# Where a layernorm's two small scaling steps run in a fused stage, and the order in which that stage issues its work

## The chip, the cores and the metric

The kernel runs on one core of one Trainium2 chip. The metric is the device time of one execution in microseconds. Three runs of the kernel before took 4185.84, 4186.37 and 4202.35 us; their median is 4186.37 us.

A core has five engines that run their own queues in order: TensorE (PE; PEld is its weight load), VectorE (DVE), ScalarE (ACT), GpSimd (POOL) and SyncE (SP), which here issues most DMAs. An instruction that waits for another engine holds up everything behind it in its own queue.

## The reference

The input is 4 sequences of 2048 tokens with 256 features, in float32. Four layers follow, each with a residual and a layernorm without weights ahead of it:

```python
def _layernorm(x, axis=-1, eps=1e-05):
    m = jnp.mean(x, axis=axis, keepdims=True)
    v = jnp.var(x, axis=axis, keepdims=True)
    return (x - m) / jnp.sqrt(v + eps)

x = x + _L0_attn_ref(_layernorm(x), ...)   # RWKV: projections, a scan over time, an FFN
x = x + _L0_ffn_ref(_layernorm(x), ...)    # 2 shared and 16 routed experts, top 4, all computed, gated
x = x + _L1_attn_ref(_layernorm(x), ...)   # Mamba: projections, convolution, selective scan with 16 states
x = x + _L1_ffn_ref(_layernorm(x), ...)    # two groups of 32 experts, top 2, tokens sorted by expert
```

## The kernel before

The tokens are cut into 16 chunks of 512 (4 sequences by 4 pieces), each held as 128 partitions by 4 groups of tokens (S = 4) by 256 features. Three phases follow one another: `rwkv_phase` (the first layer), `mixed_phase` (the second and third layers and the routing of the fourth: the fused stage that the change touches) and `grouped_phase` (the experts of the fourth layer, page by page).

In `mixed_phase` each chunk n goes through three sets of steps. `experts` loads the chunk, normalizes it ("b"), computes router gates, and takes 18 experts in 5 batches: `weights` loads (SP), `up` matmuls (PE), `gelu` (ACT, with a table load before and after), `gated` (a product on POOL), `down` (PE), `added` (DVE). `front` normalizes again ("c"), projects, convolves (`taken` on ACT, `conv` on DVE), and computes the step sizes (`soft` on ACT, `lost` and `dt` on DVE, `less` and `dx` on POOL). `back` runs the selective scan: for g and m in 4 by 4, `enter` forms the inputs c_u on POOL in two halves, `decay` computes one exponential c_da per q on ACT into a PSUM bank, `scan` (L1294) runs the recurrence on DVE in place in c_u, `add` sums over states on PE, `keep` saves the last state on ACT. `steps_in` and `inputs_in` load their inputs through SP. Then `gated` and `out_of` give the layer's output, `summed` (L1330) adds the residual, the chunk is normalized a third time ("w"), and a router with a chain of small DVE steps (`less_max`, `terms`, `largest`, `one_hot`, `rank`, `take_pages`, `place`, `note_pages`, `pick`) finds the row of each token, to which `put` (16 indirect DMAs from POOL) scatters it. In this chain ACT makes small copies: c_np (L1455) in `note_pages` is one that DVE's next step (L1461) waits for, pos_sb (L1483) in `pick` one that `put` waits for.

The order is written out by hand. `MIXED_ORDER` has for each step a list of places, one for each of its instances in a chunk: 456 places in all. Instance i of chunk n is issued at place n * 456 + entry. An entry of -343 is thus issued one chunk's length before the chunk's own start, beside the back of the chunk before. Every engine gets its instructions in this order, so places modulo 456 show what stands next to what once the stage has filled. PSUM banks (8) go round in the order of issue too: a step that takes a bank waits for the reader of the tile that was there. c_u has three buffers.

Each of the three layernorms takes `stats` on DVE (one bn_stats and bn_aggr for each of the 4 groups of tokens), then `scale`, which calls `moments` (L860 to L868): on 128 x 4 numbers it adds epsilon to the variance (rs, L863) and negates the mean (sh, L865) on DVE, then raises rs to the power -0.5 (L866) and multiplies sh by it (L867) on POOL. `normed` (L871) applies both on ACT.

Of the kernel before, what the change touches and what calls it, by code (L numbers as in the profile page):

```python
# [9 lines left out]
F32 = mybir.dt.float32  # L10
I32 = mybir.dt.int32
AF = mybir.ActivationFunctionType
ALU = mybir.AluOpType
# [4 lines left out]
P = 128  # L18
# [3 lines left out]
S = TC // P  # L22
# [6 lines left out]
EPS_LN = 1e-5  # L29
# [20 lines left out]
def bcast_dram(ap, n):  # L50

    run = 1
    for s in ap.shape:
# [4 lines left out]


MIXED_ORDER = {  # L60
    "experts.load": [-1147],
    "b.stats": [-1088, -1083, -1082, -1077],
    "b.normed": [-1054, -1040, -1031, -1032],
    "b.scale": [-1060],
    "b.turn": [-1021, -1018],
    "experts.turned": [-1011, -1002],
    "experts.logit": [-985],
    "experts.logit_out": [-982],
    "experts.logit_turn": [-957],
    "experts.less_max": [-925],  # L70
    "experts.terms": [-921],
    "experts.total": [-914],
    "experts.largest": [-907],
    "experts.taken": [-889],
    "experts.weighted": [-870],
    "experts.gate_turn": [-865],
    "experts.gate_out": [-846],
    "experts.weights": [-860, -852, -800, -755, -714, -648, -639, -608, -516, -419],
    "experts.gates_in": [-810, -764, -685, -624, -500],
    "experts.up": [  # L80
        -830, -816, -815, -735, -748, -720, -719, -652, -642, -635, -631, -541, -540, -579,
        -535, -484, -472, -470,
    ],
    "experts.gelu": [-813, -718, -625, -534, -461],
    "experts.gated": [-793, -1407, -711, -702, -620, -613, -527, -521, -459, -449],
    "experts.down": [
        -787, -783, -768, -759, -681, -672, -657, -645, -595, -589, -577, -567, -504, -497,
        -520, -514, -389, -388, -417, -415,
    ],
    "experts.added": [-757, -747, -663, -641, -572, -552, -476, -482, -369, -395],  # L90
    "c.stats": [-365, -362, -347, -363],
    "c.normed": [-333, -321, -326, -328],
    "c.scale": [-343],
    "c.turn": [-315, -287],
    "front.turned": [-304, -281],
    "front.project": [-273, -259, -260, -243],
    "front.taken": [-265, -238, -226, -219],
    "front.conv": [-254, -252, -250, -234, -230, -227, -223, -221, -213, -209, -206, -198],
    "front.silu_x": [-194],
    "front.b_of": [-153],  # L100
    "front.b_out": [-137],
    "front.dt_of": [-159, -158, -75, -68, 0, 2, 114, 115],
    "front.soft": [-147, -145, -57, -51, 19, 26, 143, 146],
    "front.lost": [-135, -46, 38, 154],
    "front.less": [-131, -36, 51, 156],
    "front.dt": [-122, -31, 78, 172],
    "front.dx": [-115, -23, 142, 217],
    "front.put": [-107, -105, 49, -18, 105, 158, 300, 239],
    "back.b_in": [-37, -129, -101, -72],
    "back.res_of": [20, 29, 14, 22],  # L110
    "back.taken_res": [28, 62, 33, 90],
    "back.silu_res": [170],
    "back.gated": [178, 244, 374, 480],
    "back.steps_in": [-104, -89, 55, 59, 167, 173, 301, 343],
    "back.inputs_in": [-92, -40, 53, 54, 179, 219, 242, 266],
    "back.enter": [
        -1, 36, -8, -7, 27, 76, 79, 86, 106, 108, 132, 134, 151, 162, 187, 188, 232, 248, 224,
        245, 254, 274, 329, 331, 318, 344, 376, 382, 363, 394, 429, 434,
    ],
    "back.decay": [  # L120
# [4 lines left out]
    ],  # L125
    "back.scan": [
# [4 lines left out]
    ],  # L131
    "back.add": [63, 69, 103, 124, 168, 208, 209, 234, 307, 320, 358, 370, 414, 435, 465, 471],
    "back.keep": [72, 81, 104, 118, 159, 215, 228, 251, 310, 305, 353, 373, 418, 444, 469, 473],
    "back.out_of": [567, 577, 488, 506],
    "back.summed": [593, 530],
    "back.store": [638],
    "w.stats": [595, 616, 603, 601],
    "w.normed": [702, 708, 713, 712],
    "w.scale": [679],
    "w.turn": [719, 721],  # L140
    "back.turned": [728, 732],
    "back.logit": [740],
    "back.less_max": [751],
    "back.terms": [758],
    "back.shares": [762],
    "back.largest": [768, 778],
    "back.one_hot": [772, 786],
    "back.count": [817],
    "back.rank": [818],
    "back.take_pages": [825],  # L150
    "back.place_pages": [831],
    "back.note_pages": [846],
    "back.place": [845],
    "back.pick": [853, 859],
    "back.put": [
        856, 863, 869, 908, 946, 970, 983, 987, 1007, 1062, 1078, 1097, 1111, 1115, 1117, 1124,
    ],
}

# [620 lines left out]
def mixed_phase(ctx, tc, cm, nb, nt, x_in, x_out, edge, pos, wgt, xs, w):  # L780
# [11 lines left out]
    nc = tc.nc  # L792
# [13 lines left out]
    wp = ctx.enter_context(tc.tile_pool(name="c_w", bufs=1))  # L806
# [28 lines left out]
    nc.vector.tensor_scalar_mul(am, am, -1.0)  # L835
    one = vp.tile([P, 1], F32, name="c_one")
    nc.vector.memset(one, 1.0)
    few = wp.tile([P, 1], F32, name="c_few")
    nc.vector.memset(few, -0.5)
    past = wp.tile([P, nb, G, NCONV - 1], F32, name="c_past")  # L840
    nc.vector.memset(past, 0.0)
    state = wp.tile([P, nb, G, NM, NC], F32, name="c_state")
# [17 lines left out]
    def moments(mv, name):  # L860

        rs = sm.tile([P, S], F32, name=f"{name}_rs")
        nc.vector.tensor_scalar_add(rs, mv[:, :, 1], EPS_LN)  # L863
        sh = sm.tile([P, S], F32, name=f"{name}_sh")
        nc.vector.tensor_scalar_mul(sh, mv[:, :, 0], -1.0)  # L865
        nc.gpsimd.tensor_tensor(rs, rs, few.to_broadcast([P, S]), ALU.pow)  # L866
        nc.gpsimd.tensor_tensor(sh, sh, rs, ALU.mult)  # L867
        return rs, sh  # L868

# [681 lines left out]
    for n in range(nb * nt):  # L1551
        c = {}
# [227 lines left out]
def layers(tc, nb, nt, w, out):  # L1780
# [5 lines left out]
    with (  # L1786
# [158 lines left out]
```

## Time and profile before

| | before |
|---|---|
| median of three runs | 4186.37 us (4185.84 to 4202.35) |
| the profiled execution | 4192.52 us; span 4190.7 us, clock 0.948 |
| busy share of the span | PE 90%, PEld 50%, DVE 80%, ACT 63%, POOL 76% |
| first phase, 0 to 1190 us | PE busy 1055, DVE 1051, POOL 951, ACT 685 us |
| fused stage once full, 1629 to 2900 us | of 1271 us: PE 1222, DVE 1212, POOL 1186, ACT 1029 us, clock 1.00 |
| last phase, 3550 to 4190 us | of 640 us: PE 545, DVE 281, POOL 264, ACT 194 us; DMA 260 GB/s |

Durations are those of one profiled execution. "Idle before" is time in which the engine stood still ahead of a group of instructions, and the arrow names what ended most of it. Waits that happen inside an instruction count as busy.

### The profile page before, as it was taken

To read this page: it belongs to the slowest core of one execution; us is meant where nothing else is said; L and a number is where in the kernel's file an instruction comes from. 1 tells how busy PE (TensorE), PEld (TensorE's weight loads), DVE (VectorE), ACT (ScalarE), POOL (GpSimd) and SP (SyncE) were. 2 spreads that over 40 slices of the span, in tenths; PEclk is the share of its full clock that TensorE was granted. 3 is DMA by queue.
4 is the path that set the end of the run, shared out by engine and by line. 5 is a ranking of instruction groups with operands and counts; after the bars stand their busy time and mean duration, and the time that the engine had idled before them with its cause. 6 is when DMAs were issued, how large, how long until landed. Compare 5 with 4: busy or idle time off the path is not lost. (4 is left out here: it accounts for less than half of the span.)

```text
span 4190.7 us, 49205 instructions
## 1 busy us (share of the span) xinstructions
PE 3753.3 (90%) x15360; PEld 2102.6 (50%) x15360; DVE 3363.2 (80%) x4824; ACT 2619.9 (63%) x4863; POOL 3182.3 (76%) x1955
## 2 busy tenths in 40 slices
PE   5799999999997999999999999999999764997986
PEld 1244444544454545545455454554545321886875
DVE  6988888888941489999999999999999996354444
ACT  4656556565643688887888778887788762332322
POOL 7978878788721588999999999999999895154245
PEclk8899999999998999999999999999999876999998
DMA  7666666767723555455555555545555334698787
GB/s 209 177 193 165 184 171 163 192 166 188 177 65 126 165 175 190 167 174 178 185 202 169 170 180 185 194 170 177 172 194 178 118 131 166 233 302 307 242 266 227
DMA packets 400259, 774.60 MB, mean 185 GB/s; under 512 B 36416, under 2 KB 238080, under 8 KB 374400
## 3 DMA queue, kind: packets, MB, share of 16 engines
q1 hardware_dynamic: 299280, 612.92, 47.5%
q10 hardware_dynamic: 76144, 91.38, 6.5%
q0 software_dynamic: 24576, 67.14, 4.5%
q8 instruction: 126, 2.06, 0.2%
q14 instruction: 133, 1.09, 0.1%
HBM read 577.32 MB, written 193.99 MB: 184 GB/s over the span
## 5 line engine op out<-in xcount | busy, mean ns | idle before, releaser
L1294 DVE TENSOR_TENSOR_SCAN c_u<-c_da,c_state,c_u 128x512 f32<-128x512 f32 x1024 | 1255.9, 1265 | 51.8 <-ACT c_da L1288 41.6
L1280 POOL TENSOR_TENSOR c_u<-c_dxr,c_bb 128x1024 f32<-128x1024 f32 x512 | 1198.4, 2363 | 36.4 <-ACT c_state L1300 23.3
L1288 ACT ACTIVATE c_da<-c_dtr,c_A 128x512 f32<-128x512 f32 x1024 | 684.4, 686 | 134.3 <-DVE c_u L1294 71.4
L550 POOL TENSOR_TENSOR a_vb<-a_vb,a_k 128x2048 f32<-128x2048 f32 x128 | 579.2, 4538 | 79.7 <-DMA a_vb<-a_vd 78.2
L560 DVE TENSOR_TENSOR_SCAN a_sc<-a_d,a_sc,a_vb 128x512 f32<-128x512 f32 x512 | 623.9, 1265 | 10.5 <-ACT a_sc L556 7.9
L1074 PE MATMUL b_acc<-b_w,b_act 128*128 128x256 f32 x2304 | 543.7, 385 | 22.1 <-POOL b_act L1067 10.9
L1049 PE MATMUL b_pu<-b_y,b_w 128*128 128x512 f32 x1152 | 533.2, 602 | 19.4 <-DVE c_dt L1199 12.6
L1746 POOL DMA_INDIRECT d_y<-d_ys,pos_sb x256 | 247.6, 967 | 364.2 <-DVE d_xt L1645 111.5
L1074 PEld LDWEIGHTS b_acc<-b_w,b_act 128*128 128x128 f32 x2304 | 425.6, 190 | 180.8 <-issue 78.5
L1306 PE MATMUL p_y<-c_u,c_red 128*32 128x512 f32 x2048 | 338.5, 626 | 73.0 <-DVE c_u L1294 54.0
L1067 POOL TENSOR_TENSOR b_act<-b_act,b_gb 128x1024 f32<-128x1024 f32 (+1 forms) x144 | 303.4, 2117 | 107.7 <-ACT b_act L1057 95.4
L1049 PEld LDWEIGHTS b_pu<-b_y,b_w 128*128 128x128 f32 x1152 | 211.3, 190 | 284.9 <-issue 183.6
L1496 POOL DMA_INDIRECT xs_dr<-w_n,pos_sb x256 | 254.9, 996 | 106.2 <-ACT pos_sb L1483 51.9
L1663 PE MATMUL d_pw<-d_w,d_xt 128*128 x1280 | 300.0, 383 | 29.3 <-DMA d_w<-in_experts 15.5
L568 DVE TENSOR_TENSOR a_sc<-a_sc,p_Wr 128x2048 f32<-128x2048 f32 x128 | 290.4, 2280 | 15.3 <-PE p_Wr L458 13.7
L1663 PEld LDWEIGHTS d_pw<-d_w,d_xt 128*128 128x128 f32 x1280 | 237.5, 192 | 67.1 <-issue 32.5
L1169 PE MATMUL p_dt<-c_xs,c_wdt 128*128 128x512 f32 x512 | 237.7, 603 | 3.9 <-ACT b_act L1057 2.4
L699 PE MATMUL p_f<-a_h,a_w 128*128 128x512 f32 x512 | 237.3, 603 | 0.3 <-ACT a_h L694 0.3
L715 PE MATMUL a_pf<-a_w,a_act 128*128 128x256 f32 x1024 | 235.9, 382 | 0.0
L1756 DVE SCALAR_TENSOR_TENSOR d_x<-d_y,wgt_sb,d_x 128x256 f32<-128x256 f32 x256 | 120.3, 483 | 132.9 <-DMA d_y<-d_ys,pos_sb 103.1
L715 PEld LDWEIGHTS a_pf<-a_w,a_act 128*128 128x128 f32 x1024 | 192.2, 190 | 65.8 <-issue 41.8
L451 POOL TENSOR_TENSOR a_mix<-a_mix,a_h 128x1024 f32<-128x1024 f32 x80 | 159.6, 1998 | 65.5 <-ACT a_mix L446 65.4
(254 smaller groups left out, 6412.4 us busy)
## 6 DMA issues: line engine op xcount, KB each, us to landing
a_vb<-a_vd SPq DMA_DIRECT2D x128, 1024.0 KB
c_dtr<-c_sd SPq DMA_DIRECT2D x256, 256.0 KB
c_dxr<-c_sd SPq DMA_DIRECT2D x256, 256.0 KB
b_gb<-b_gd SPq DMA_DIRECT2D x48, 1024.0 KB
xs_dr<-zero_sb SPq DMA_DIRECT2D x32, 1280.0 KB
d_xb<-xs_dr SPq DMA_DIRECT2D x80, 512.0 KB
d_ys<-d_yb ACTq DMA_DIRECT2D x80, 512.0 KB
b_w<-in_up SPq DMA_DIRECT2D x48, 512.0 KB
```

Of the source, the lines that this page charges most:

```text
L550: nc.gpsimd.tensor_tensor(vb, vb, c["k"][:, half : half + 1, :].to_broadcast([P, NC, TC]), ALU.mult)
L560: nc.vector.tensor_tensor_scan(sc[:, j, 1 : TC + 1], c["d", half], c["vb", half, js][:, j, :], sc[:, j, 0:1], ALU.mult, ALU.add,)
L568: nc.vector.tensor_tensor(sc[:, :, 0:TC], sc[:, :, 0:TC], r.unsqueeze(1).to_broadcast([P, NC, TC]), ALU.mult,)
L715: nc.tensor.matmul(c["pf2", s], c["a"][:, fc, s * P : (s + 1) * P], w2[:, fc, :], start=(fc == 0), stop=(fc == n_fc - 1),)
L1049: nc.tensor.matmul(c["pu", e], c["w", e, 0][:, kc * P : (kc + 1) * P], c["f"][:, kc, :], start=(kc == 0), stop=(kc == KC - 1),)
L1067: nc.gpsimd.tensor_tensor(a, a, c["gb", k][:, 2 * i : 2 * i + n, :], ALU.mult)
L1074: nc.tensor.matmul(c["pa", k, h][:, s % 2, :], c["act", k][:, i, s * P : (s + 1) * P], c["w", e, 1], start=(i == 0), stop=(i == len(batche ...
L1280: nc.gpsimd.tensor_tensor(c["u", g, m][:, r, :], c["dxr", g][:, r, :], c["bb", m].to_broadcast([P, 2, TC]), ALU.mult,)
L1288: nc.scalar.activation(c["da", g, m, q], c["dtr", g][:, q, :], AF.Exp, scale=am[:, i : i + 1])
L1294: nc.vector.tensor_tensor_scan(u, c["da", g, m, q], u, state[:, b, g, m, q : q + 1], ALU.mult, ALU.add)
L1306: nc.tensor.matmul(c["acc", g][q * QB : (q + 1) * QB, :], red, c["u", g, m][:, q, :], start=(m == 0), stop=(m == NM - 1), skip_group_check ...
L1663: nc.tensor.matmul(c["pw", h][:, j % 2, :], c["xt"][:, kc, j * P : (j + 1) * P], part(j, kc), start=(kc == 0), stop=(kc == KC - 1),)
```

## The change

The two steps rs + epsilon and -sh move from VectorE to ScalarE: rs as an Identity activation with epsilon from a second column of c_few as its bias, sh as a multiplication. Powers and product stay on GpSimd. In addition `MIXED_ORDER` is replaced by another order of the same 456 places. The lists that the text below speaks of are shown; nearly all others differ by a few places as well.

```diff
 MIXED_ORDER = {
...
-    "b.stats": [-1088, -1083, -1082, -1077],
+    "b.stats": [-1093, -1078, -1082, -1088],
...
-    "b.scale": [-1060],
+    "b.scale": [-1065],
...
-    "experts.logit_out": [-982],
+    "experts.logit_out": [-968],
...
-    "experts.terms": [-921],
+    "experts.terms": [-932],
-    "experts.total": [-914],
+    "experts.total": [-918],
-    "experts.largest": [-907],
+    "experts.largest": [-912],
...
-    "experts.weights": [-860, -852, -800, -755, -714, -648, -639, -608, -516, -419],
+    "experts.weights": [-905, -851, -818, -743, -707, -612, -585, -553, -544, -501],
...
-    "experts.gelu": [-813, -718, -625, -534, -461],
+    "experts.gelu": [-803, -717, -621, -530, -458],
...
-    "c.stats": [-365, -362, -347, -363],
+    "c.stats": [-358, -353, -354, -351],
...
-    "c.scale": [-343],
+    "c.scale": [-341],
...
-    "back.steps_in": [-104, -89, 55, 59, 167, 173, 301, 343],
+    "back.steps_in": [-101, -48, 53, 74, 156, 163, 347, 349],
-    "back.inputs_in": [-92, -40, 53, 54, 179, 219, 242, 266],
+    "back.inputs_in": [-79, -73, 26, 65, 189, 198, 259, 266],
-    "back.enter": [
-        -1, 36, -8, -7, 27, 76, 79, 86, 106, 108, 132, 134, 151, 162, 187, 188, 232, 248, 224,
-        245, 254, 274, 329, 331, 318, 344, 376, 382, 363, 394, 429, 434,
-    ],
+    "back.enter": [
+        23, 42, 4, 14, 35, 57, 68, 70, 71, 78, 116, 137, 142, 178, 182, 183, 249, 277, 244, 261,
+        283, 289, 319, 344, 313, 351, 353, 358, 367, 395, 417, 441,
+    ],
-    "back.decay": [
-        40, 18, 48, 43, 6, 12, 25, 56, 64, 35, 77, 84, 88, 80, 92, 73, 98, 100, 122, 127, 149,
-        131, 133, 163, 107, 174, 186, 176, 200, 207, 195, 180, 225, 261, 279, 289, 241, 236,
-        238, 275, 313, 283, 294, 326, 332, 354, 342, 339, 365, 368, 395, 387, 423, 424, 379,
-        406, 446, 441, 432, 401, 431, 457, 439, 459,
-    ],
+    "back.decay": [
+        41, 16, 46, 48, 3, 27, 21, 54, 69, 40, 82, 81, 99, 76, 93, 89, 58, 126, 112, 124, 147,
+        111, 119, 171, 139, 159, 185, 187, 206, 212, 201, 188, 232, 257, 270, 288, 237, 231,
+        224, 276, 315, 279, 297, 322, 304, 338, 340, 356, 370, 376, 393, 389, 420, 425, 396,
+        426, 451, 449, 429, 401, 431, 457, 439, 462,
+    ],
-    "back.scan": [
-        45, 30, 57, 46, 21, 16, 31, 65, 70, 44, 83, 85, 110, 89, 116, 101, 117, 120, 126, 136,
-        161, 138, 140, 181, 171, 184, 190, 189, 216, 220, 214, 211, 269, 268, 290, 296, 253,
-        259, 278, 282, 324, 293, 315, 338, 346, 359, 348, 356, 393, 380, 404, 402, 426, 427,
-        422, 421, 450, 460, 445, 409, 437, 464, 466, 467,
-    ],
+    "back.scan": [
+        45, 38, 59, 56, 20, 33, 25, 72, 79, 44, 97, 86, 118, 90, 100, 114, 121, 127, 123, 125,
+        161, 141, 157, 186, 179, 164, 191, 197, 217, 221, 216, 210, 267, 265, 287, 298, 263,
+        262, 272, 282, 329, 292, 314, 332, 343, 360, 345, 361, 384, 391, 402, 409, 424, 427,
+        428, 432, 453, 464, 438, 412, 447, 468, 467, 473,
+    ],
...
-    "w.stats": [595, 616, 603, 601],
+    "w.stats": [601, 667, 616, 602],
...
-    "w.scale": [679],
+    "w.scale": [682],
...
-    "back.note_pages": [846],
+    "back.note_pages": [844],
...
-    "back.put": [
-        856, 863, 869, 908, 946, 970, 983, 987, 1007, 1062, 1078, 1097, 1111, 1115, 1117, 1124,
-    ],
+    "back.put": [
+        859, 861, 870, 871, 904, 962, 974, 1025, 1047, 1077, 1086, 1104, 1111, 1120, 1125, 1132,
+    ],
@@ -835,8 +835,9 @@
     nc.vector.tensor_scalar_mul(am, am, -1.0)
     one = vp.tile([P, 1], F32, name="c_one")
     nc.vector.memset(one, 1.0)
-    few = wp.tile([P, 1], F32, name="c_few")
-    nc.vector.memset(few, -0.5)
+    few = wp.tile([P, 2], F32, name="c_few")
+    nc.vector.memset(few[:, 0:1], -0.5)
+    nc.vector.memset(few[:, 1:2], EPS_LN)
     past = wp.tile([P, nb, G, NCONV - 1], F32, name="c_past")
     nc.vector.memset(past, 0.0)
     state = wp.tile([P, nb, G, NM, NC], F32, name="c_state")
@@ -860,10 +861,10 @@
     def moments(mv, name):
 
         rs = sm.tile([P, S], F32, name=f"{name}_rs")
-        nc.vector.tensor_scalar_add(rs, mv[:, :, 1], EPS_LN)
+        nc.scalar.activation(rs, mv[:, :, 1], AF.Identity, bias=few[:, 1:2])
         sh = sm.tile([P, S], F32, name=f"{name}_sh")
-        nc.vector.tensor_scalar_mul(sh, mv[:, :, 0], -1.0)
-        nc.gpsimd.tensor_tensor(rs, rs, few.to_broadcast([P, S]), ALU.pow)
+        nc.scalar.mul(sh, mv[:, :, 0], -1.0)
+        nc.gpsimd.tensor_tensor(rs, rs, few[:, 0:1].to_broadcast([P, S]), ALU.pow)
         nc.gpsimd.tensor_tensor(sh, sh, rs, ALU.mult)
         return rs, sh
```

More of the change, by code (lines that the diff above doesn't have):

```diff
@@ L60 @@
 MIXED_ORDER = {
-    "experts.load": [-1147],
-    "b.stats": [-1088, -1083, -1082, -1077],
-    "b.normed": [-1054, -1040, -1031, -1032],
-    "b.scale": [-1060],
-    "b.turn": [-1021, -1018],
-    "experts.turned": [-1011, -1002],
-    "experts.logit": [-985],
-    "experts.logit_out": [-982],
-    "experts.logit_turn": [-957],
-    "experts.less_max": [-925],
-    "experts.terms": [-921],
-    "experts.total": [-914],
-    "experts.largest": [-907],
-    "experts.taken": [-889],
-    "experts.weighted": [-870],
@@ L76 @@
-    "experts.gate_turn": [-865],
-    "experts.gate_out": [-846],
-    "experts.weights": [-860, -852, -800, -755, -714, -648, -639, -608, -516, -419],
-    "experts.gates_in": [-810, -764, -685, -624, -500],
+    "experts.load": [-1159],
+    "b.stats": [-1093, -1078, -1082, -1088],
+    "b.normed": [-1043, -1040, -1026, -1034],
+    "b.scale": [-1065],
+    "b.turn": [-1014, -1002],
+    "experts.turned": [-1011, -993],
+    "experts.logit": [-981],
+    "experts.logit_out": [-968],
+    "experts.logit_turn": [-958],
@@ L80 @@
+    "experts.less_max": [-955],
+    "experts.terms": [-932],
+    "experts.total": [-918],
+    "experts.largest": [-912],
+    "experts.taken": [-907],
+    "experts.weighted": [-846],
+    "experts.gate_turn": [-832],
+    "experts.gate_out": [-827],
+    "experts.weights": [-905, -851, -818, -743, -707, -612, -585, -553, -544, -501],
+    "experts.gates_in": [-821, -759, -654, -575, -505],
     "experts.up": [
-        -830, -816, -815, -735, -748, -720, -719, -652, -642, -635, -631, -541, -540, -579,
@@ L82 @@
-        -535, -484, -472, -470,
-    ],
-    "experts.gelu": [-813, -718, -625, -534, -461],
-    "experts.gated": [-793, -1407, -711, -702, -620, -613, -527, -521, -459, -449],
+        -820, -816, -808, -736, -760, -719, -718, -652, -641, -638, -631, -543, -534, -577,
+        -532, -490, -470, -467,
+    ],
+    "experts.gelu": [-803, -717, -621, -530, -458],
+    "experts.gated": [-795, -1643, -709, -708, -619, -611, -522, -520, -441, -407],
     "experts.down": [
-        -787, -783, -768, -759, -681, -672, -657, -645, -595, -589, -577, -567, -504, -497,
-        -520, -514, -389, -388, -417, -415,
-    ],
@@ L90 @@
-    "experts.added": [-757, -747, -663, -641, -572, -552, -476, -482, -369, -395],
-    "c.stats": [-365, -362, -347, -363],
-    "c.normed": [-333, -321, -326, -328],
-    "c.scale": [-343],
[L94 to L112, printed above, removed]
@@ L113 @@
-    "back.gated": [178, 244, 374, 480],
-    "back.steps_in": [-104, -89, 55, 59, 167, 173, 301, 343],
-    "back.inputs_in": [-92, -40, 53, 54, 179, 219, 242, 266],
+        -772, -769, -761, -745, -679, -669, -664, -658, -596, -586, -582, -573, -493, -482,
+        -515, -513, -379, -372, -405, -404,
+    ],
+    "experts.added": [-764, -735, -667, -648, -576, -548, -469, -478, -361, -373],
+    "c.stats": [-358, -353, -354, -351],
+    "c.normed": [-328, -322, -320, -318],
+    "c.scale": [-341],
@@ new lines @@
+    "c.turn": [-307, -290],
+    "front.turned": [-302, -276],
+    "front.project": [-272, -260, -238, -241],
+    "front.taken": [-266, -234, -226, -217],
+    "front.conv": [-256, -254, -249, -231, -229, -222, -221, -215, -205, -214, -206, -201],
+    "front.silu_x": [-188],
+    "front.b_of": [-147],
+    "front.b_out": [-135],
+    "front.dt_of": [-162, -154, -71, -62, -4, 2, 106, 108],
+    "front.soft": [-151, -144, -52, -40, 30, 34, 130, 133],
+    "front.lost": [-136, -35, 39, 144],
+    "front.less": [-132, -23, 55, 150],
@@ L116 @@
+    "front.dt": [-123, -19, 64, 172],
+    "front.dx": [-110, -1, 170, 228],
+    "front.put": [-115, -106, -16, 9, 110, 175, 310, 240],
+    "back.b_in": [-83, -93, -10, 28],
+    "back.res_of": [29, 31, 13, 32],
+    "back.taken_res": [37, 43, 63, 75],
+    "back.silu_res": [162],
+    "back.gated": [168, 236, 379, 478],
+    "back.steps_in": [-101, -48, 53, 74, 156, 163, 347, 349],
+    "back.inputs_in": [-79, -73, 26, 65, 189, 198, 259, 266],
     "back.enter": [
-        -1, 36, -8, -7, 27, 76, 79, 86, 106, 108, 132, 134, 151, 162, 187, 188, 232, 248, 224,
@@ L118 @@
-        245, 254, 274, 329, 331, 318, 344, 376, 382, 363, 394, 429, 434,
+        23, 42, 4, 14, 35, 57, 68, 70, 71, 78, 116, 137, 142, 178, 182, 183, 249, 277, 244, 261,
+        283, 289, 319, 344, 313, 351, 353, 358, 367, 395, 417, 441,
     ],
     "back.decay": [
[4 rows of a table removed]
[4 rows of a table added]
     ],
     "back.scan": [
[4 rows of a table removed]
-    ],
-    "back.add": [63, 69, 103, 124, 168, 208, 209, 234, 307, 320, 358, 370, 414, 435, 465, 471],
-    "back.keep": [72, 81, 104, 118, 159, 215, 228, 251, 310, 305, 353, 373, 418, 444, 469, 473],
@@ L134 @@
-    "back.out_of": [567, 577, 488, 506],
-    "back.summed": [593, 530],
-    "back.store": [638],
-    "w.stats": [595, 616, 603, 601],
-    "w.normed": [702, 708, 713, 712],
-    "w.scale": [679],
-    "w.turn": [719, 721],
-    "back.turned": [728, 732],
-    "back.logit": [740],
-    "back.less_max": [751],
[L144 to L150, printed above, removed]
@@ L151 @@
-    "back.place_pages": [831],
-    "back.note_pages": [846],
-    "back.place": [845],
-    "back.pick": [853, 859],
[4 rows of a table added]
+    ],
+    "back.add": [67, 88, 107, 132, 173, 219, 223, 229, 306, 308, 348, 365, 418, 435, 466, 475],
+    "back.keep": [73, 87, 101, 120, 155, 214, 273, 238, 317, 307, 352, 371, 423, 444, 474, 480],
+    "back.out_of": [578, 585, 492, 503],
+    "back.summed": [587, 516],
+    "back.store": [614],
+    "w.stats": [601, 667, 616, 602],
+    "w.normed": [702, 708, 703, 709],
+    "w.scale": [682],
@@ L155 @@
+    "w.turn": [712, 725],
+    "back.turned": [734, 740],
+    "back.logit": [741],
+    "back.less_max": [751],
+    "back.terms": [752],
+    "back.shares": [755],
+    "back.largest": [767, 779],
+    "back.one_hot": [774, 787],
+    "back.count": [818],
+    "back.rank": [828],
+    "back.take_pages": [830],
+    "back.place_pages": [837],
+    "back.note_pages": [844],
+    "back.place": [842],
+    "back.pick": [854, 862],
     "back.put": [
-        856, 863, 869, 908, 946, 970, 983, 987, 1007, 1062, 1078, 1097, 1111, 1115, 1117, 1124,
+        859, 861, 870, 871, 904, 962, 974, 1025, 1047, 1077, 1086, 1104, 1111, 1120, 1125, 1132,
```

## The prediction

> **What bounds the kernel now.** I read the page first (slices, costliest groups), then busy times by stage, then the groups of VectorE and GpSimd over four chunks of the fused stage, then single stretches in order of time.
>
> The fused stage runs from about 1190 to 3550 us and repeats one order 16 times. Its last residual add (L1330) of a chunk comes every 131.6 to 132.0 us between 1593 and 3305 us: 13 equal intervals. Busy time in two chunks, and over five such windows (columns: window, length, PE, PEld, DVE, ACT, POOL, clock, DMA share, GB/s):
>
> ```profile
> 1855.90:2119.40 263.50, 253.16 (x1069) 133.71 (x1069) 251.55 (x392) 214.09 (x395) 246.51 (x145) 1.00 0.53 181
> sum 1317.40, PE 1265.97 PEld 668.49 DVE 1257.34 ACT 1070.67 POOL 1232.49; mean PE 253.19 PEld 133.70 DVE 251.47 ACT 214.13 POOL 246.50
> ```
>
> Per chunk of 131.75 us: PE 126.6, DVE 125.7, POOL 123.25, ACT 107.1. Three engines are nearly full and each loses the rest to waits for the others; ScalarE has 24.7 us to spare. PE's figure overstates its need, since b_acc matmuls of 379 ns start 216 ns apart; so I go by VectorE and GpSimd. Their groups over four chunks (busy, mean ns, then idle time before and what ended it), VectorE first:
>
> ```profile
> L863 DVE TENSOR_SCALAR c_rs<-bn_mv 128x4 f32<-128x4 f32 x4 | 7.6, 1903 | 0.0
> L863 DVE TENSOR_SCALAR w_rs<-bn_mv 128x4 f32<-128x4 f32 x4 | 3.1, 785 | 0.0
> L1294 DVE TENSOR_TENSOR_SCAN c_u<-c_da,c_state,c_u 128x512 f32<-128x512 f32 x257 | 315.9, 1265 | 7.5 <-ACT c_da L1288 7.2
> L1461 DVE TENSOR_TENSOR c_X<-c_Y,consts_sb 64x128 f32<-64x128 f32 x4 | 1.2, 300 | 8.9 <-ACT c_np L1455 8.9
> ```
>
> ```profile
> L1280 POOL TENSOR_TENSOR c_u<-c_dxr,c_bb 128x1024 f32<-128x1024 f32 x129 | 302.3, 2365 | 3.9 <-ACT c_state L1300 1.9 <-DVE c_before L1419 1.4
> L1496 POOL DMA_INDIRECT xs_dr<-w_n,pos_sb x64 | 64.0, 999 | 18.1 <-issue 11.4 <-ACT pos_sb L1483 5.0 <-DVE w_sh L865 0.7
> L1195 POOL TENSOR_TENSOR c_e<-c_ln,c_e 128x512 f32<-128x512 f32 x16 | 20.3, 1270 | 7.0 <-DVE c_e L1189 7.0
> L866 POOL TENSOR_TENSOR b_rs<-b_rs,c_few 128x4 f32<-128x4 f32 x4 | 4.0, 1008 | 2.9 <-DVE b_sh L865 2.9
> ```
>
> A step on 128x4 numbers takes 1.9 us in c_rs and 0.16 us in b_rs. The timeline says why: it starts while GpSimd's c_u product runs and ends when that ends (1976.91 + 4.67 = 1981.58). VectorE's lines, then GpSimd's:
>
> ```profile
> 1979.72 1.90 DVE L863 TENSOR_SCALAR c_rs<-bn_mv 128x4 f32<-128x4 f32 x1
> 1981.53 0.16 DVE L865 TENSOR_SCALAR c_sh<-bn_mv 128x4 f32<-128x4 f32 x1
> ```
>
> ```profile
> 1976.91 4.67 POOL L1280 TENSOR_TENSOR c_u<-c_dxr,c_bb 128x1024 f32<-128x1024 f32 x2
> 1981.69 1.04 POOL L866 TENSOR_TENSOR c_rs<-c_rs,c_few 128x4 f32<-128x4 f32 x1
> ```
>
> So that time counts as busy and is a wait. [...]
>
> **The change part by part.** Places below are folded: entry p modulo 456, the length of the order.
>
> *The six small steps leave VectorE.* From the start of each pair to the next instruction: c 1979.72 to 1981.60, 1.88; w 0.75; b 0.15. Sum 2.8 us a chunk off VectorE, on the path since it is 95% busy. Both are slow in 13 chunks of 16.
>
> *They join ScalarE.* Six steps of about 0.2 us (rows of that size there: c_state 128x4 0.187, wgt_sb 128x8 0.205): 1.2 us into 24.7 us of spare time, so 0; without that cover 1.2 x 13 = 16 us. The normalization (L871) already runs Identity with no table load, and the new queue has as many loads as the old. The new wait, ScalarE for the moments, stands behind terms, which waits for a later VectorE step, for b; for w behind taken[1] and 4 VectorE steps after its last moment; for c see the rival. One memset more at the start is 0.06 us.
>
> [...]
>
> *The new order and VectorE's three gaps.* The largest is L1461, 2.2 us a chunk. ScalarE, then VectorE:
>
> ```profile
> 2058.62 1.28 ACT L1059 ACT_TABLE_LOAD   x1
> 2059.92 0.69 ACT L1288 ACTIVATE c_da<-c_dtr,c_A 128x512 f32<-128x512 f32 x1
> 2060.55 0.26 ACT L963 COPY b_lt<-b_logit 128x128 f32<-128x128 f32 x1
> 2060.70 0.69 ACT L1288 ACTIVATE c_da<-c_dtr,c_A 128x512 f32<-128x512 f32 x1
> 2061.32 0.21 ACT L1474 ACTIVATE c_full<-c_Y 128x64 f32<-128x64 f32 x1
> ```
>
> ```profile
> 2062.06 0.31 DVE L1461 TENSOR_TENSOR c_X<-c_Y,consts_sb 64x128 f32<-64x128 f32 x1 [2.23 <-ACT c_np L1455]
> ```
>
> Two decays and logit_out stand between gelu[3] and the copies that VectorE waits for. In the new order they stand behind note_pages (decay[51] 387 to 389, logit_out 386 to 400, decay[54] 379 to 396; note_pages 388): 2061.32 - 2059.92 = 1.4 us less. What remains, 0.8, is gelu[3] itself, whose last matmul still waits for gated[2]'s bank. The gap of 0.94 before scan[61] follows gelu[4]; there scan[62] (1.18 us) now runs ahead of scan[61], and terms, which held gelu[4] back for VectorE, moves from 447 to 436: 0.9 gone. Before scan[30], 0.86 behind gelu[1], the w moments (0.4 + 0.18) move in: 0.5 gone. VectorE: 131.75 - 2.8 - 1.4 - 0.9 - 0.5 = 126.1 us.
>
> *GpSimd is next.* Its 8.5 us of idle time a chunk hold waits for other engines of (3.3 + 5.0 + 0.7 + 7.0 + 2.9) / 4 = 4.7; the other 3.8 are issue and gaps between instructions. It does the same work, so 123.25 + 3.8 = 127.0 is its floor, above VectorE's 126.1. Of the 4.7 I keep a third, 1.6: c_e and c_before wait for VectorE, which is now less late; pos_sb and b_sh keep part. Bounds 0 and 4.7.
>
> *Queues moved past.* In SP's queue weights[1], which waits for matmuls, now stands ahead of inputs_in[3] and steps_in[3] (60 to 61, 54 to 65, 59 to 74). inputs_in[3] was issued 28.8 us before its first reader, steps_in[3] 14.4; both have cover, 0. GpSimd's put[3] and put[4] move ahead of enter[2], put[7] and put[8] behind enter[9]; the count of puts is the same, 0. Ramps at both ends keep about their lengths: 0, between -10 and +10 us.
>
> **Sum.** Chunk 127.0 + 1.6 = 128.6, 3.15 less than 131.75; x 13 = 41 us. The profiled execution took 4192.5 us (span 4190.7), so 4151.5 by its own time; it stands 6.1 above the median of 4186.4, which becomes 4145. The case spans chunks of 127.0 (-62) to 130.1 (-21), with the ramps about 4112 to 4165.
>
> **Rivals.** *The gain is absorbed.* PE stays at 126.6 busy plus new waits for banks (up[14] one place behind gated[2] instead of three, decay[35] now behind turned[1]), or GpSimd keeps all 4.7 us of waits: 131.0 us a chunk, -10, 4177; it spans 4165 to 4207. For it: PE is the fullest row. Against: its overlap above.
>
> *Slower: GpSimd waits at c_rs for ScalarE.* Today it waits there for VectorE, 0.1 us. Now c.scale (115) stands in ScalarE's queue behind gelu[0], moved from 99 to 109 (3 x 0.6 + 2 x 1.28 = 4.4 us), and two decays (1.25), while GpSimd gets there sooner: four puts fewer from enter[2] on, enter[8] and enter[9] at 71 and 78 instead of 106 and 108. Behind the wait stand enter[10] and gated[0], then scans and down[0]. Worst 4.4 + 1.25 + 0.4 = 6.0 us; with 127.0 and 1.6, 134.6, or +2.9 x 13 = +37; with all 4.7 kept, 137.7, +77. Likeliest 4240. It decides once that wait exceeds 131.75 - 128.6 = 3.15 us. Against it: enter[8] needs a c_u buffer that keep[1] or add[1] frees, which holds GpSimd to the scans' pace, and the fullest engine tends to come last to a meeting.
>
> **How the numbers follow.** About 0.5% (21 us) is what a measurement of this kernel can tell from no change. Forecast 0.71, absorbed 0.17, slower 0.12; each lies in one class. The time is the forecast's, 4145. The range 4112 to 4195 leaves out the slower rival, the top of the absorbed case and a gain beyond the floor, together about 0.2.
>
> **What would show it.** Right: chunks 127 to 130 us apart; no TENSOR_SCALAR on VectorE for rs and sh, 0.2 us each on ScalarE; L1461's idle under 1 us a chunk; GpSimd idle under 7 us a chunk. Wrong: c_rs on GpSimd waiting more than 3 us for ScalarE, PE or scans idle for a new releaser, or a chunk still near 131.7.

## The result, and the profile after

The changed kernel took 4175.4 us against 4191.4 us (medians of 19 runs each): ratio 0.9959, 95% interval 0.9941 to 0.9978, some 17 us faster. The forecast was 41 us faster.

Runs of one kernel spread by some tens of us, while the chunk hardly moves: after and two variants that came out equal lie within 0.04 us, though each kernel has one profile only. The spread goes with the granted clock: of 29 runs of before in one set the shortest took 4155.1 us at a mean clock of 0.952, the longest 4207.0 at 0.948. In the full stage the profiles of before, after, ops_only, order_only and c_on_vector show a clock of 0.99 to 1.00; before's shows 0.90, 0.93 and 0.96 in the three parts of the first phase (to 400, 800 and 1190 us) and 0.96 from 3560 to 4140 us. The difference is thus taken to lie outside the full stage, an inference from one profile of each. So the experiments below are read by three times from the profile of each, all of the last residual add of a chunk (L1330 before, L1331 after): when the first chunk has it (the start), when the last chunk has it (the end), and the chunk, which is the mean of the 13 intervals that follow the first chunk's add.

| | start | chunk | end |
|---|---|---|---|
| before | 1593.0 | 131.71 | 3518.7 |
| after | 1601.5 | 129.75 | 3500.0 |

The end is 18.7 us earlier: 13 x 1.96 = 25.5 from the chunk, 1.7 from the emptying pipeline, less 8.5 that the start is later. Busy times after, in two chunks and over five such windows (columns: window, length, PE, PEld, DVE, ACT, POOL, clock, DMA share, GB/s):

```profile
1858.80:2119.60 260.80, 252.12 (x1072) 135.27 (x1076) 247.29 (x379) 215.65 (x407) 246.18 (x145) 1.00 0.55 182
sum 1301.00, PE 1261.13 PEld 676.80 DVE 1235.79 ACT 1078.44 POOL 1230.51; mean PE 252.23 PEld 135.36 DVE 247.16 ACT 215.69 POOL 246.10
```

Per chunk VectorE is busy 123.6 us (125.7 before), ScalarE 107.8 (107.1), GpSimd 123.05 as before. Only ScalarE, which has 22 us to spare, has become fuller, yet the chunk is over 1 us longer than forecast. The groups over four chunks tell what the idle time is now (busy, mean ns, then idle time before and what ended it):

```profile
L1295 DVE TENSOR_TENSOR_SCAN c_u<-c_da,c_state,c_u 128x512 f32<-128x512 f32 x256 | 313.7, 1266 | 9.3 <-POOL c_u L1281 6.5 <-ACT c_da L1289 2.2
L1281 POOL TENSOR_TENSOR c_u<-c_dxr,c_bb 128x1024 f32<-128x1024 f32 x128 | 299.2, 2359 | 4.8 <-DMA c_dxr<-c_sd 2.8 <-ACT c_state L1301 1.1
...
L1196 POOL TENSOR_TENSOR c_e<-c_ln,c_e 128x512 f32<-128x512 f32 x16 | 20.3, 1270 | 0.1
...
L867 POOL TENSOR_TENSOR c_rs<-c_rs,c_few 128x4 f32<-128x4 f32 x4 | 4.2, 1042 | 2.4 <-ACT c_sh L866 2.4
...
L1462 DVE TENSOR_TENSOR c_X<-c_Y,consts_sb 64x128 f32<-64x128 f32 x4 | 1.2, 300 | 3.1 <-ACT c_np L1456 3.1
...
L864 ACT ACTIVATE c_rs<-bn_mv,c_few 128x4 f32<-128x4 f32 x4 | 1.1, 282 | 0.0
```

The old gaps shrank as the prediction had it: L1462 waits 3.1 / 4 = 0.8 us a chunk (2.2 before), scans for ScalarE's decays 0.55 (1.8), GpSimd's c_e for VectorE nothing (1.75). New ones stand in their place: scans wait for GpSimd (6.5 / 4 = 1.6), GpSimd's c_rs for ScalarE (0.6), GpSimd's c_u for a load (0.7). The c_rs wait in order of time, ScalarE first, then the last stats on VectorE, then GpSimd:

```profile
2238.75 1.28 ACT L1058 ACT_TABLE_LOAD   x1
2240.04 1.82 ACT L1058 ACTIVATE b_act<-b_pu 128x512 f32<-128x512 f32 x3
...
2241.88 1.28 ACT L1060 ACT_TABLE_LOAD   x1
2243.17 1.30 ACT L1289 ACTIVATE c_da<-c_dtr,c_A 128x512 f32<-128x512 f32 x2
2244.41 0.28 ACT L864 ACTIVATE c_rs<-bn_mv,c_few 128x4 f32<-128x4 f32 x1
2244.60 0.19 ACT L866 ACTIVATE c_sh<-bn_mv 128x4 f32<-128x4 f32 x1
```

```profile
2241.57 0.18 DVE L921 BATCH_NORM_AGGREGATE bn_mv<-bn_st 128x2 f32<-128x6 f32 x1
```

```profile
2242.90 1.01 POOL L1497 DMA_INDIRECT xs_dr<-w_n,pos_sb  x1 [0.16 <-issue]
2244.78 1.04 POOL L867 TENSOR_TENSOR c_rs<-c_rs,c_few 128x4 f32<-128x4 f32 x1 [0.88 <-ACT c_sh L866]
```

The moments were ready at 2241.75. ScalarE took them up at 2244.41, after gelu[0] with its two table loads and two decays; GpSimd, free at 2243.91, waited 0.88 us. That is the place of the rival "slower", at little more than a quarter of the price that it needed to decide. (This is one chunk; the mean of eight is 0.9 us too, 7.0 / 8 in a view below.)

### The profile page after: what moved, and what is told of

The parts are those of the page before. It is cut to its first block, busy times and chain, and to the rows that moved or that the text cites. A ratio compares the mean times of both kernels' runs of the same rounds, so it can differ in the third digit from the quotient of the medians.

```text
span 4178.2 us, 49110 instructions
## 1 busy us (share of the span) xinstructions
PE 3752.3 (90%) x15360; PEld 2117.0 (51%) x15360; DVE 3326.1 (80%) x4729; ACT 2633.8 (63%) x4959; POOL 3177.4 (76%) x1955
## 3 DMA queue, kind: packets, MB, share of 16 engines
q14 instruction: 130, 1.06, 0.1%
## 4 chain that ended last, share of the span: by engine, by line
PE 34%; DVE 12%; ACT 9%; POOL 7%; issue 5%; DMA 3%; another core or an unknown queue 1%; ACTq 0%; SPq 0%; POOLq 0%; DVEq 0%
PE b_pu L1050 6%; PE b_acc L1075 6%; DVE c_u L1295 6%; PE d_pw L1664 5%; POOL c_u L1281 3%; PE p_y L1307 3%; PE d_po L1696 3%; PE p_dt L1170 3%; PE p_res L1260 2%; ACT c_da L1289 2%; PE d_pt L1638 1%; PE p_out L1324 1%; ACT b_act L1058 1%; ACT L1060 1%; DVE p_in L1142 1%
## 5 line engine op out<-in xcount | busy, mean ns | idle before, releaser
L1664 PEld LDWEIGHTS d_pw<-d_w,d_xt 128*128 128x128 f32 x1280 | 238.3, 192 | 60.2 <-issue 24.3
```

Source lines behind the costliest of these rows:

```text
L1664: nc.tensor.matmul(c["pw", h][:, j % 2, :], c["xt"][:, kc, j * P : (j + 1) * P], part(j, kc), start=(kc == 0), stop=(kc == KC - 1),)
```

## The experiments

The expectations name five theories. A: VectorE sets the chunk, so what leaves it is gained. B: the loop of VectorE and GpSimd sets it, with GpSimd's waits. C: as soon as one wait goes another takes its place. D: one chain through w_rs, ScalarE and TensorE sets it. E, formed after the first eight of these kernels: ScalarE's late answer at c paces the new order and cancels VectorE's relief. All measured values:

| kernel | start | chunk | end | ratio to before (95%) |
|---|---|---|---|---|
| before | 1593.0 | 131.71 | 3518.7 | 1 |
| after | 1601.5 | 129.75 | 3500.0 | 0.9959 (0.9941 to 0.9978) |
| ops_only | 1602.8 | 131.34 | 3523.2 | 0.9989 (0.9955 to 1.0024) |
| order_only | 1592.7 | 129.76 | 3491.8 | 0.9912 (0.9877 to 0.9946) |
| sp_back | 1602.3 | 129.79 | 3499.6 | 0.9987 (0.9958 to 1.0016) |
| puts_late | 1601.7 | 129.76 | 3500.4 | 0.9974 (0.9942 to 1.0007) |
| oo_wscale | 1593.2 | 132.27 | 3522.2 | 1.0046 (1.0016 to 1.0075) |
| af_wscale | 1602.7 | 129.85 | 3499.9 | 0.9983 (0.9957 to 1.0008) |
| af_cscale | 1599.0 | 129.04 | 3488.4 | 0.9947 (0.9919 to 0.9974) |
| notes_only | 1593.1 | 130.82 | 3506.0 | 0.9967 (0.9940 to 0.9993) |
| c_on_vector | 1595.0 | 128.48 | 3475.7 | 0.9917 (0.9886 to 0.9949) |
| oo_sp | 1590.9 | 129.31 | 3483.7 | 0.9925 (0.9898 to 0.9952) |
| af_c2 | 1596.9 | 129.28 | 3489.2 | 0.9952 (0.9924 to 0.9981) |
| ops_notes | 1601.7 | 130.46 | 3510.0 | 0.9978 (0.9950 to 1.0007) |
| c_vec_load_late | 1590.8 | 128.87 | 3476.5 | 0.9920 (0.9889 to 0.9950) |
| old_c_vec | 1593.5 | 131.18 | 3511.2 | 0.9966 (0.9939 to 0.9994) |

### Each part alone

ops_only is before's order with the diff's edit of `moments` and `few`. order_only is after's `MIXED_ORDER` with before's `moments` and `few`.

> The order of before, with epsilon and sign put on by ScalarE: the first part of the change alone. Theory A (VectorE sets the chunk, so what leaves it is gained): the chunk of 131.75 us loses the 2.8 us of the six steps, or a little less where a wait for GpSimd returns, to 129.0 to 129.5; 13 chunks make 29 to 36 us, so some 32 us faster than before, and more than the whole change brought (17). Theory B (the loop of VectorE and GpSimd sets it: GpSimd has 123 us of work and keeps its waits): what VectorE saves it then waits for GpSimd or ScalarE; chunk 131 to 131.5, 3 to 10 us faster. If ScalarE answers late at the c moments (GpSimd's c_rs step waiting for ScalarE by over 1 us), B's lower end.

> The new order, with epsilon and sign still on VectorE: the second part alone. Theory A: the chunk of after, 130.0, gets the 2.8 us of VectorE back: 132.8, so about 1 us a chunk or 14 us slower than before, and with the longer ramp some 20 us slower: the new order by itself would be a loss. Theory B (the GpSimd waits set the chunk): 130.0 to 131, 10 to 20 us faster than before, as VectorE's 2.8 us fall into times when it would wait.

The new order alone has the chunk of the whole change, 129.76, and its end is 8.2 us earlier, because the start is. The edit alone takes 0.37 us off the chunk and makes the start 9.8 us later; its end is 4.5 us later than before. Theory A fails on both; B's chunk holds for ops_only (131 to 131.5) and is 0.2 us too long for order_only (130.0 to 131). Two views say why. VectorE's waits in ops_only over eight chunks (us in total, times, longest):

```profile
DVE c_u L1295 <- POOL c_u L1281: 6.5, 16, 0.5
DVE c_x L1331 <- PE p_out L1324: 5.6, 9, 0.6
```

Neither is there before: 1.5 us a chunk of what left VectorE came back as waits for GpSimd and TensorE. And the groups of order_only over four chunks:

```profile
L863 DVE TENSOR_SCALAR b_rs<-bn_mv 128x4 f32<-128x4 f32 x4 | 4.2, 1058 | 0.0
L863 DVE TENSOR_SCALAR c_rs<-bn_mv 128x4 f32<-128x4 f32 x4 | 0.9, 233 | 0.0
L863 DVE TENSOR_SCALAR w_rs<-bn_mv 128x4 f32<-128x4 f32 x4 | 0.8, 198 | 0.0
```

In the new order the c_rs step takes 0.23 us instead of 1.90, though nobody touched it, and the b_rs step 1.06 us instead of 0.16. In before's trace these steps take over 0.17 us only beside a product of GpSimd (last section); so the new order has, an inference from that, moved c_rs out of such a product in most chunks and b_rs into one. The two terms of the prediction were not independent.

That the chunks of order_only and after are equal is no sign that moving the steps does nothing. GpSimd is idle 7.05 us a chunk in both, but with other waits. In order_only (eight chunks) it waits 9.6 us for ScalarE at the experts' product (`gated`, b_act) and 3.8 us for VectorE at c_dx; in after the first is 5.6, the second is gone, and 7.0 us at c_rs have come in. c_vec_load_late, below, takes this apart.

Most of the late start has one place. GpSimd at the first chunk's c moments, in after and then in order_only:

```profile
1372.59 1.01 POOL L867 TENSOR_TENSOR c_rs<-c_rs,c_few 128x4 f32<-128x4 f32 x1 [13.91 <-ACT c_rs L864]
```

```profile
1365.68 1.01 POOL L866 TENSOR_TENSOR c_rs<-c_rs,c_few 128x4 f32<-128x4 f32 x1 [8.02 <-DVE c_sh L865]
```

The stats were there at 1368.1 in after and 1365.4 in order_only. VectorE answered within 0.3 us. ScalarE stood in a gelu that waited for TensorE's matmuls (1.01 us ahead of its last part, at 1370.30), and came 4 us later. Of the 6.9 us between the two lines 2.7 are thus there before ScalarE's answer; 0.8 of these are older than the stage, since the first chunk's b stats end at 1195.2 us in after and at 1194.4 in order_only. With the c pair on VectorE (c_vec_load_late, below) the whole late start is gone.

### The load, and the puts

```diff
sp_back (on after):    experts.weights[1]  -851 -> -837.5    (61 -> 74.5, behind steps_in[3])
puts_late (on after):  back.put[9], [10]   1077, 1086 -> 1095.3, 1095.6   (behind enter[15])
```

> After, with the load weights[1] put behind inputs_in[3] and steps_in[3] in SyncE's queue again, as before the change (one place moved). GpSimd's wait for that load at enter[9] (0.5 us a chunk in after) should go in every theory. Theory A and B alike give at most that on the chunk: 129.5 for 130.0, 6 us of 13 chunks, if GpSimd's lateness there reaches VectorE (its scans 18 and 19 stand behind enter[9]); 0 if GpSimd only waits longer at the next place, the c moments.

> After, with put[9] and put[10] (1 us of GpSimd each) moved behind enter[13] to enter[15]. VectorE waits 1.65 us a chunk for enter[13] at scan[26] in after. Theory B (that loop sets the chunk): enter[13] comes up to 2 us sooner, the wait goes and the chunk falls by 1 to 1.6 us to 128.4 to 129, 13 to 21 us faster than after. Theory C (TensorE or another wait sets it): the wait at scan[26] goes and another takes its place at once; within 5 us of after.

Both chunks stay at 129.8. GpSimd's waits over eight chunks, after and then sp_back:

```profile
POOL c_rs L867 <- ACT c_sh L866: 7.0, 7, 1.3
...
POOL c_u L1281 <- DMA c_dxr<-c_sd: 3.5, 6, 1.3
```

```profile
POOL c_rs L867 <- ACT c_sh L866: 10.6, 8, 1.4
```

The wait for the load is gone from sp_back's list, and the wait for ScalarE behind it grew from 0.9 to 1.3 us a chunk: GpSimd came sooner to a meeting whose time ScalarE sets. In puts_late VectorE's wait for GpSimd at the scans is 13.7 us in eight chunks as against 13.1, so the puts did not hold enter[13], and neither theory was put to the test: the wait itself stayed.

### The w moments earlier

```diff
oo_wscale (on order_only), af_wscale (on after):   w.scale  682 -> 668.5   (226 -> 212.5)
```

> The new order with epsilon and sign on VectorE (order_only), and one place moved: w.scale from 682 to 668.5, so that GpSimd's w_rs and w_sh stand ahead of put[14] and put[15] instead of behind them. In order_only ScalarE waits 3.1 us a chunk for those two numbers before it normalizes w_n, and the chain of waits runs through that place: puts, w_rs, w_n, silu of x, gelu[1], front.put, a scan, then some 68 us of TensorE without a gap. Theory D (one chain through GpSimd, ScalarE and TensorE sets the chunk, no single engine's sum): the chain loses 2 to 3 us; chunk 127 to 128 for 130.0, and 26 to 39 us faster than order_only. Theory A or B (VectorE, or GpSimd's sum of work and waits): GpSimd does the same work, chunk 129.5 to 130, within 6 us of order_only.

> After (epsilon and sign on ScalarE), with the same one place moved: w.scale from 682 to 668.5. Theory D: 130.0 falls to 127 to 128, as far as ScalarE's two steps are then not late themselves; 26 to 39 us faster than after. Theory A or B: within 6 us of after. If VectorE's 2 us are worth something once the chain is shorter, this kernel's chunk is below that of oo_wscale; if not, equal.

Theory D falls: after's chunk stays, order_only's grows by 2.5 us, which no theory had. The same move is harmless with ScalarE and costly with VectorE. oo_wscale in order of time, VectorE and then GpSimd:

```profile
2139.91 4.24 DVE L863 TENSOR_SCALAR w_rs<-bn_mv 128x4 f32<-128x4 f32 x1
```

```profile
2139.43 4.68 POOL L1067 TENSOR_TENSOR b_act<-b_act,b_gb 128x1024 f32<-128x1024 f32 x2
```

The step on 128x4 numbers takes 4.24 us and ends 0.04 us after the second of two GpSimd products. Over eight chunks w_rs takes 4.47 us on average where order_only's took 0.26: 4.2 us more of this step on VectorE come with 2.5 us more of chunk. oo_wscale's total is by its ratio 19 us over before's, 16 more than its end accounts for. That part lies behind the stage, where its profile shows a clock of 0.94 as against 0.96 in before's (3560 to 4140 us); its cause stays open.

### ScalarE's answer at c sooner

```diff
af_cscale (on after):  c.scale  -341 -> -347.5   (115 -> 108.5, ahead of gelu[0])
af_c2: the same, and   c.stats  [-358, -353, -354, -351] -> [-360.8, -360.6, -360.4, -360.2]
```

> After, with c.scale moved from 115 to 108.5, that is ahead of gelu[0] and its two decays in ScalarE's queue. GpSimd's wait for ScalarE at c_rs (0.8 us a chunk, and 13.9 us once, near 1360 us, where the first chunk's c_rs waits behind a gelu that waits for TensorE; VectorE answered there after 8.0 us) should go. Expected of the start: the first chunk's last residual add at 1593 to 1595 us instead of 1601.5, 7 to 8 us faster at the end, whatever sets the steady chunk. Theory B: besides that up to 0.8 us a chunk, 129.2; theory D: the chunk stays at 129.8 to 130.

> After with c.scale ahead of gelu[0] (as in af_cscale) and the four c stats moved on VectorE from 98 to 105 to 95.2 to 95.8, ahead of scan[10] and scan[14]. In af_cscale gelu[0] and the two decays behind c.scale waited for VectorE's last stats, and VectorE then 3.1 us a chunk for those decays. Theory E: the stats are there 2.5 us sooner, so that wait falls to about 1 us; chunk 127.8 to 128.6 for 129.0 in af_cscale, and the start recovers, first residual add at 1594 to 1596. Theory C: scan[10] and scan[14], 2.3 us later, hold add[2] and GpSimd's buffers, chunk 129 to 130.

af_cscale's chunk falls by 0.71, as theory B had it: c_rs no longer waits, and scans no longer wait for GpSimd. But they now wait for ScalarE (VectorE's waits, eight chunks):

```profile
DVE c_u L1295 <- ACT c_da L1289: 24.9, 16, 2.5
```

gelu[0] and the decays behind it stand behind c.scale, which waits for VectorE's stats: 3.1 us a chunk. The start recovers by 2.5 us only, where 7 to 8 were expected, although c_rs follows its stats there at once (1364.9 to 1365.0 us); what holds the start then was not found. af_c2 brings the scans' wait to 2.1 us and loses it elsewhere: its chunk of 129.28 is what theory C had, and theory E's 127.8 to 128.6 is missed. With ScalarE in this place either GpSimd waits behind gelu[0], or gelu[0] waits behind VectorE.

### VectorE at c, ScalarE at b and w

c_vec_load_late is after with this `moments`, c_on_vector adds sp_back's edit, old_c_vec has the old order. oo_sp is order_only with sp_back's edit.

```diff
+        if name == "c":
+            nc.vector.tensor_scalar_add(rs, mv[:, :, 1], EPS_LN)
+            nc.vector.tensor_scalar_mul(sh, mv[:, :, 0], -1.0)
+        else:
             nc.scalar.activation(rs, mv[:, :, 1], AF.Identity, bias=few[:, 1:2])
             nc.scalar.mul(sh, mv[:, :, 0], -1.0)
```

> sp_back (the new order, weights[1] behind the two loads) with the c moments' epsilon and sign on VectorE again and those of b and w on ScalarE. In sp_back GpSimd waits 1.3 us a chunk at c_rs for ScalarE, which is behind gelu[0], and nothing else was gained there. Theory E (the late answer of ScalarE at c paces the new order and is what cancels VectorE's relief): that wait goes, VectorE pays 0.3 us for c_rs as in order_only; chunk 128.7 to 129.2 for 129.8, the start 8 us earlier (first chunk's last residual add at 1593 instead of 1602); 20 us faster than after. Theory C (another wait is next at once): chunk 129.6 to 130, only the 8 us of the start.

> order_only (the new order, all epsilon and sign on VectorE) with weights[1] behind the two loads. The same edit brought nothing in after, where GpSimd's 0.5 us only moved to the c_rs wait for ScalarE. Here no such wait stands behind it. Theory E: GpSimd's wait for the load (0.6 us a chunk) goes and is gained, chunk 129.2 to 129.4 for 129.8, 6 to 8 us. Theory C: 129.7 to 129.9, nothing.

> After with the c moments' epsilon and sign on VectorE and those of b and w on ScalarE, the order as it is in after (weights[1] ahead of the two loads). Theory E (the c_rs wait for ScalarE alone covers the gain): chunk 129.0 to 129.2, that is 0.5 to 0.7 over c_on_vector (128.48), the GpSimd wait for the load back at 0.5 to 0.6; the start as in c_on_vector, first residual add at 1595. If the two waits only count together (either one hides the other): 129.7, as in after and sp_back.

Theory E holds in all three; the two chunks with the c pair on VectorE are 0.1 to 0.2 us shorter than its ranges. Moving the c pair alone back to VectorE takes 0.88 us off after's chunk and 10.7 off its start; the end is 23.5 us earlier. Of the 10.7 us 2.9 are older than the stage: the first chunk's b stats end at 1192.3 us there and at 1195.2 in after. The c_rs wait is gone from GpSimd's list, and VectorE's scans wait for GpSimd half as long. After, then c_vec_load_late, eight chunks:

```profile
DVE c_u L1295 <- POOL c_u L1281: 13.1, 8, 1.7
```

```profile
DVE c_u L1299 <- POOL c_u L1285: 6.6, 8, 1.0
```

That is 0.8 us a chunk, about what the chunk loses. Against order_only, c_vec_load_late has only the b and w pairs on ScalarE, and its chunk is 0.89 us shorter. So in the new order these two pairs gain 0.89 us and the c pair loses 0.88: that is why after and order_only are equal.

The load's edit, worth nothing in after, is worth 0.39 us a chunk with the c pair on VectorE (c_on_vector against c_vec_load_late, though with a start 4.2 us later, 2.7 of them older than the stage, so the ends are 0.8 us apart) and 0.45 on order_only. c_on_vector is the version that beats both kernels: 4144.7 us against 4183.0 for before, its end 24.3 us ahead of after's. Its busy times over five windows of two chunks:

```profile
sum 1287.00, PE 1256.29 PEld 675.65 DVE 1235.71 ACT 1076.30 POOL 1230.44; mean PE 251.26 PEld 135.13 DVE 247.14 ACT 215.26 POOL 246.09
```

GpSimd does the same 123.04 us of work in 128.7: 5.7 us idle against 7.05 in after.

### The old order

```diff
notes_only (on before), ops_notes (on ops_only):   back.decay[51]  387 -> 390.3    back.decay[54]  379 -> 396.5
```

> Before, with decay[51] and decay[54] alone moved behind note_pages (387 to 390.3, 379 to 396.5). VectorE waits 2.2 us there for ScalarE's copies, and some 1.2 us of that should go. Theory A: the chunk falls by 1.2, to 130.5, 16 us faster. Theory D (VectorE is not on the chain that sets the chunk): 131.5 to 131.75, within 4 us of before.

> The old order with both parts that were tried alone: epsilon and sign on ScalarE (alone 131.34, 0.37 less) and decay[51] and decay[54] behind note_pages (alone 130.82, 0.89 less). If both take time from one chain, they add: 130.45. If VectorE's relief only shows once that gap is gone (theory A), 128.5 to 129.5. If they share one slack, 130.8.

> The old order with the c moments on VectorE and those of b and w on ScalarE. In ops_only (all six on ScalarE, chunk 131.34) VectorE has the 1.9 us of the c_rs step off its hands and waits 0.8 us a chunk more for GpSimd and 0.7 for TensorE. Theory A (VectorE's time there is on the path): the 1.9 us come back, chunk 131.7 or more. Theory E (those 1.9 us are GpSimd's pace, so VectorE waits for it with or without the step, while ScalarE's answer behind gelu[0] costs 0.36): chunk 131.0 to 131.3, and the start at 1593 instead of 1602.8, some 10 us faster than ops_only.

In notes_only VectorE's wait at L1461 falls by 0.8 us (2.2 to 1.4) where 1.2 were expected, GpSimd's for pos_sb, a later copy of the same ScalarE, by as much (1.3 to 0.5), and the chunk by 0.89: these waits for ScalarE are on the path, and which of the two counts is not told apart. The gains add in ops_notes (0.37 + 0.89 = 1.26 expected, 1.25 measured). In old_c_vec the slow step is back:

```profile
L866 DVE TENSOR_SCALAR c_rs<-bn_mv 128x4 f32<-128x4 f32 x8 | 15.2, 1898 | 0.0
```

and the chunk is 0.16 us shorter than in ops_only, with ops_only's waits for GpSimd and TensorE gone from VectorE's list. So those 1.9 us were worth less than the 0.36 us of GpSimd's wait that replaced them. The start is back at 1593.5. Against before, old_c_vec has the b and w pairs alone on ScalarE: they gain 0.53 us (131.71 to 131.18), most of the 0.66 us by which VectorE's busy time falls. w_rs too was slow in before (0.79 us; it ended 0.03 to 0.04 us after a GpSimd product), so a wait inside a step is not worthless everywhere.

## Why the prediction was wrong

Chunk 128.6 was forecast, 129.75 came: 1.15 x 13 = 15 us. The start was forecast unchanged and came 8.5 us later. Together 23.5 us. c_vec_load_late's end is earlier than after's by the same amount through one pair of steps; that the sums agree is in part chance, since it is made of 11.4 us of chunk, 10.7 of start (2.9 of them older than the stage) and 1.2 of the emptying pipeline.

The step that failed is the prediction's treatment of GpSimd's waits. Its sum went by GpSimd, 127.0 + 1.6, since VectorE's own figure of 126.1 was lower. GpSimd's work came as forecast (123.05 us for 123.25), and so did its issue and gaps (3.65 for 3.8). Its waits for other engines came to 3.4 us (27.2 in eight chunks) where a third of the old 4.7, 1.6, had been kept, and the largest of them, c_rs for ScalarE, had been left out of the sum and given to a rival. Term by term:

- *"Six small steps leave VectorE", 2.8 us on the path:* that VectorE is 95% busy does not put its time on the path. The old order gives 0.37 us for all six: 0.53 for the pairs of b and w, less 0.16 for the c pair, whose 1.9 us were a wait for GpSimd's product; removing it does not make GpSimd faster. The new order takes 1.2 of the six steps' 3.3 busy us away by itself (2.1 in order_only). In it the b and w pairs are worth 0.89 us, or 129.31 - 128.48 = 0.83 with the load mended (oo_sp against c_on_vector), for 1.1 us less of VectorE's busy time (124.6 to 123.6).
- *"They join ScalarE, 0":* their 0.28 and 0.19 us are hidden, as said. The wait was not. The rival "slower" named the place and was right in mechanism; its 3.15 us needed to decide became 0.9, enough to cancel the relief but not to turn the sign. That case, a wait that eats only the relief, had no share of the forecast's own sum.
- *"Both have cover, 0" for the loads:* 28.8 us of cover in the old order are no cover in the new one, where GpSimd waits 0.4 to 0.7 us a chunk. Worth about 0.4 us where no later wait swallows it, 0 in after.
- *"Residual waits 1.6 us":* GpSimd's idle time is 7.05 us a chunk, not 5.4. The old waits went almost entirely, more than forecast. c_rs 0.9, the load 0.4, gated 0.7 and b_gate 0.5 (eight-chunk list) are new or larger. With c_rs and the load mended (c_on_vector) it is 5.7, and the chunk 128.5 to 128.7, the forecast. Scaling old waits down said nothing of new ones. After's chunk lies inside the span that the case gave itself, near its long end, but that end of 130.1 is not worked out: with all 4.7 us kept, the bound that the text names, it would be 131.7.
- *"Ramps 0, between -10 and +10":* +8.5 at the start, 0.8 of it older than the stage and the rest from the same c pair, less 1.7 at the end: inside the bound and on its bad side. In the filling pipeline ScalarE's queue waits for TensorE, so what stands behind gelu is later than in the full stage: in after ScalarE's c_rs began 4.1 us after its stats in the first chunk, and 2.7 us after them in the chunk of the full stage shown above.
- *VectorE's three gaps:* right in size. L1461 went to 0.8 us as worked out, and the scans' two gaps, with 0.4 us left over by the prediction, to 0.55. A new wait of 0.7 us at L1377 came in (5.7 in eight chunks). notes_only lost 0.8 us of the L1461 gap and as much of GpSimd's pos_sb wait for 0.89 us of chunk. The new order by itself brings 2 us a chunk, though what of it comes from each gap was not taken apart.
- *"131.75 us", "13 equal intervals":* the first of the 13 is 131.0 us and their mean 131.71, which changes the sum by 0.5 us.
- *The rival "absorbed":* its end result, near -10, is the nearer one, its reason only in part: GpSimd did keep waits, though other ones, and TensorE was not tested apart. It is busy 125.6 of 128.7 us in c_on_vector; whether it sets the next limit stays open.

The length of the steps does not explain the miss either: in after they take 0.28 + 0.19 = 0.47 us a pair on ScalarE, which has 22 us to spare, and b and w gain by the move.

## What to carry to other kernels

A short step given to the engine with spare time can cost what stands ahead of it in that engine's queue, not its own length (at c in after a wait of 0.9 us a chunk, with 0.47 us of steps): look at what it is queued behind when its inputs are ready, in the full pipeline and in its filling, and move it only where that is nothing long. Busy time that is a wait for another engine's instruction has no fixed price: at c in the old order 1.9 us less of it brought at most 0.2 us, at w in oo_wscale 4.2 us more of it cost 2.5. Price it by an experiment in its own place. When an order is replaced, list the new waits, not only what becomes of the old ones.

## What the runs showed of the hardware

A TENSOR_SCALAR of 128x4 numbers on VectorE took 0.145 us (c_on_vector's c_rs), 0.23 (order_only's c_rs), 1.06 (its b_rs), 1.90 (before's c_rs), and 4.47 us on average for w_rs in oo_wscale. In before's trace 29 of the 48 steps b_rs, c_rs and w_rs ran beside a product of GpSimd: they took 0.42 to 2.21 us and ended 0.02 to 0.04 us after it. The other 19 took 0.14 to 0.17 us. In the chunk of oo_wscale shown above the step began 0.48 us after the first of two products of one line and ended 0.04 us after the second, so it did not come in between the two. Scans, of which many run beside such products, took 1.25 to 1.29 us each, all 1024 of before.

The totals of one kernel moved by more than most of these edits do (52 us between the shortest of the 29 runs of before, at a mean clock of 0.952, and the longest, at 0.948), while the clock in the full stage was 0.99 to 1.00 in the profiles named above. So a change of this size is better read from the profile of its stage than from a few totals.
